# Four changes around TensorE in a four-layer graph network: degrees by quarters, layer 3's exponentials through DRAM, a weight and a bias moved to ScalarE, and a planner that prices changes of use by pairs

## The chip, the cores and the metric

The kernel runs on one core of a Trainium2 chip. The core has five engines with instruction queues of their own: TensorE (PE) multiplies matrices into accumulators (PSUM), VectorE (DVE) and ScalarE (ACT) do elementwise work and reductions, GpSimd (POOL) takes small powers here, and SyncE (SP) issues all transfers between DRAM and the on-chip memory (SBUF), which 16 DMA engines carry out. Engines wait for each other by semaphores. The metric is the device time of one execution in microseconds, the median of several runs.

## The reference, cut to what matters

64 graphs, independent of each other, with 256 nodes of 256 features and a 256 x 256 weighted adjacency each, pass through four layers. Each layer is `x = layernorm(x + layer(x, adj))`. All is float32.

```
layer 0: X, q, k = lrelu(x W_lin + b), lrelu(x W_q), lrelu(x W_k)          # 4 heads of 64
         A = adj * sigmoid(q k^T / 8); deg = sum over neighbours of A
         dis = deg^-0.5 where deg > 0, else 0; Y = layernorm(dis A dis X)
layer 1: masked attention, 8 heads of 32: q = x Wq + bq, softmax, v, Wo
layer 2: h = (eps x + adj x) W1 + b1                                       # 1024 wide
         h = silu(h * rsqrt(mean(h^2) + 1e-6) * rms_weight); h W2 + b2
layer 3: Wh = h W; e = leakyrelu(s1[i] + s2[j]), masked; softmax; attention Wh
         gelu(layernorm(...))
```

## The kernel before

**Staging.** A graph's arrays are tiles of 128 partitions. A 256 x 256 array is one tile of 128 x 512 (two blocks of 128 nodes, or of 128 features, side by side). All weights are loaded once. For each graph `graph()` (from L239) records some 300 operations, for all 64 graphs, and nothing is issued yet. An operation has an engine, a cost in ns, what it writes and reads, and for PE a *mode*: "full" (all of the array), "rows" (heads of 32 or 64 features on strips of rows, L433 and L515), "columns" (results of 32 or 64 partitions on strips of columns, L450, L476, L551) or "transpose" (a product with the identity).

**Order.** `Plan.order()` (L95 to L164) then plays the recorded operations through a model of the engines and writes down the order: at each step it takes, of all operations that have their inputs, the one that can start first. A change of PE's mode costs `CHANGE[mode]`, by the mode that is left (L23, L114). `AFTER` and `ITSELF` are the delays until another engine, or the same, may use a result. Buffers come from pools with fixed numbers of slots (`SLOTS`, L34: 42 of 128 x 516 words, 8 accumulators, 8 places in DRAM for bounces, and others), and an operation that needs a slot waits for a free one. ACT's tables (sigmoid, exponential, silu, gelu) are changed in *turns*, four for each round of graphs; layer 1 of a graph runs two rounds after its layer 0, layer 2 after five, layer 3 after seven (`ROUND`, L32). Loads may run at most `AHEAD` turns ahead (L29). So some eight graphs are in flight at different layers, and each engine gets one long fixed list that it works off in order. Every engine's list is fixed at build time; only semaphores hold it up.

**The parts that the change touches.** (Lines of the kernel before.)

- *Layer 0's degrees*, L448 to L464. VectorE has added the node blocks of A (`added`, two heads in each of two tiles). PE multiplies them by a 128 x 32 block of ones, one matmul of 256 columns for each head, into a strip of 32 partitions each (L450): in `ps`, the 32 partitions of a strip hold the same row of 256 degrees. ACT copies it to SBUF (L453), PE transposes it in two blocks (L458), and VectorE reads the degrees by node from every 32nd column of that accumulator (L462, L464), with POOL's power -0.5 (L463) between.
- *Layer 1's queries*, L499 to L502: PE's product and VectorE's addition of the bias per feature.
- *Layer 2*, L589 to L628. For eight blocks of 128 hidden features PE multiplies (L594), ACT adds the bias and brings the block to `hT` (L599), ACT squares two blocks at once (L602), VectorE adds the squares (L605, L607), PE takes the mean over features (L612), POOL the power (L616), and PE spreads the factors over the partitions of an accumulator `pr` (L621). VectorE multiplies each block by the RMS weight (a value per partition) and `pr` (L624), and ACT takes the silu of four blocks (L628). PE's second product (L637) follows.
- *Layer 3's exponentials*, L663 to L672: ACT, VectorE and ACT make `e`; PE transposes it in four blocks (L264), ACT copies the result to SBUF (L300), and PE multiplies it with `Wh` (L320, `ps<-v,eT`).
- *Transposition through DRAM*, `far_transposed` (L272): VectorE transposes the 32 x 32 blocks of a tile (L276), four transfers write them to DRAM (L282), four read them back with the blocks in their transposed places (L286), in runs of 32 words. Layer 3's input x3 goes this way in all but the last three graphs (L643).

Of the kernel before, what the change touches and what calls it, by code (L numbers as in the profile page):

```python
# [11 lines left out]
OP = mybir.AluOpType  # L12

P = 128
# [5 lines left out]
PE_MM, PE_TR = 432, 109  # L20
AFTER = {"PE": 230, "DVE": 150, "ACT": 190, "POOL": 180, "SP": 3000}
ITSELF = {"PE": 0, "DVE": 95, "ACT": 110, "POOL": 60, "SP": 0}
CHANGE = {"full": 0, "rows": 100, "columns": 140, "transpose": 60}  # L23
TABLE_LOAD = 1430

DMA_KB, DMA_SEEN = 4, 1900

WORDS = {"s": 516, "d": 1024, "b": 2048, "c": 32, "p": 512, "h": 1024}
AHEAD = 12  # L29
NEAR = 1, 1, 3  # L30

ROUND = 0, 2, 5, 7  # L32
# [43 lines left out]
class Plan:  # L76
# [9 lines left out]
    def op(self, engine, cost, fn, w=(), r=(), turn=None, mode="full", after=None, size=0):  # L86
        pair = lambda x: x if isinstance(x, tuple) else (x, None)
        w, r = [pair(x) for x in w], [pair(x) for x in r]
        op = Op(engine, cost, fn, w, r, self.graph, turn, mode, after, size)
        op.table = turn is not None and engine == "ACT"  # L90
        if op.table:
            self.turns[turn] = self.turns.get(turn, 0) + 1
        self.ops.append(op)

    def order(self):  # L95
        for i, op in enumerate(self.ops):
            op.index = i
        for op in reversed(self.ops):
            op.due = min((nxt.due for nxt in op.after), default=4 * (min(op.graph + ROUND[3], self.graphs - 1 + TAIL[3]) + 1))
            if op.turn is not None:  # L100
                op.due = min(op.due, op.turn)
        clock = {e: 0.0 for e in AFTER}
        self.free = {k: [(0.0, i) for i in range(n)] for k, n in SLOTS.items()}
        turns, left = sorted(self.turns), dict(self.turns)
        turn, loaded, mode, moved = 0, None, "full", 0.0
        ready = {op for op in self.ops if not op.waits}
        done = []
        self.busy = {e: 0.0 for e in AFTER}
        while ready:
            best = None  # L110
            for op in ready:
                if (op.due - AHEAD if op.first else op.turn or 0) > turns[turn]:
                    continue
                start = max(clock[op.engine] + (CHANGE[mode] if op.engine == "PE" and op.mode != mode else 0), op.ready)  # L114
                need = {}
                for v in op.values:
                    if v.slot is None:
                        need[v.kind] = need.get(v.kind, 0) + 1
                for kind, n in need.items():
                    free = self.free[kind]  # L120
                    if len(free) < n:
                        break
                    start = max(start, sorted(free)[n - 1][0])
                else:
                    key = start, op.due, op.graph, op.index
                    if best is None or key < best[0]:
                        best = key, start, op
            if best is None:
                raise RuntimeError(f"the plan is stuck at {len(done)} of {len(self.ops)}")
            _, start, op = best  # L130
            op.start = start
            ready.discard(op)
            if op.table and op.turn != loaded:
                op.start, loaded = op.start + TABLE_LOAD, op.turn
            if op.engine == "PE":
                mode = op.mode
            end = clock[op.engine] = op.start + op.cost
            op.landed = end + op.seen
            if op.engine == "SP":
                moved = max(moved, end) + op.size * DMA_KB  # L140
                op.landed = max(op.landed, moved + DMA_SEEN)
            self.busy[op.engine] += op.cost
            done.append(op)
            op.takes = [v for v in op.values if v.slot is None]
            for v in op.takes:
                self.free[v.kind].sort()
                v.slot = self.free[v.kind].pop(0)[1]
            for v in op.values:
                v.uses -= 1
                v.end = max(v.end, op.landed)  # L150
                if not v.uses:
                    self.free[v.kind].append((v.end, v.slot))
            for nxt in op.after:
                nxt.waits -= 1
                nxt.ready = max(nxt.ready, end + ITSELF[op.engine] if nxt.engine == op.engine != "SP" else op.landed)
                if not nxt.waits:
                    ready.add(nxt)
            if op.table:
                left[op.turn] -= 1
                while turn < len(turns) - 1 and not left[turns[turn]]:  # L160
                    turn += 1
        assert len(done) == len(self.ops)
        self.span = max(op.start + op.cost for op in done)
        return sorted(done, key=lambda op: op.start)  # L164
# [7 lines left out]
def weights(plan, nc, c, t):  # L172
# [38 lines left out]

    v = const("eps_id", [P, P])
    op("DVE", 200, lambda v=v: nc.vector.tensor_scalar(v.t, c.ident, c.eps2.t[:, 0:1], None, op0=OP.mult), [v], [c.eps2])


    ps, v = Value("p", "ps"), const("c1", [P, D])
# [22 lines left out]
def graph(plan, nc, c, t, out, b):  # L239
# [206 lines left out]
           [added[i]], [(att, 2 * i), (att, 2 * i + 1)])  # L446

    def fn(ps=ps):  # L448
        for h in range(H0):
            pe.matmul(ps.t[h * 32:(h + 1) * 32, :N], c.ones, two(added[h // 2])[:, h % 2], start=True, stop=True)  # L450
    op("PE", PE_MM, fn, [ps], added, mode="columns")
    deg = Value("s", "deg")
    op("ACT", 258, lambda ps=ps: act.copy(deg.t[:, :N], ps.t[:, :N]), [deg], [ps])  # L453
    pd = Value("p", "ps")

    def fn():
        for n in range(NB):
            pe.transpose(pd.t[:, n * P:(n + 1) * P], deg.t[:, n * P:(n + 1) * P], c.ident)  # L458
    op("PE", 2 * PE_TR, fn, [pd], [deg], mode="transpose")
    dp, dis = Value("c", "dp"), Value("c", "dis")  # L460
    D8 = lambda: pd.t[:, :N].rearrange("p (g k) -> p g k", k=32)[:, :, 0]
    op("DVE", 50, lambda: dve.tensor_scalar(dp.t[:, :8], D8(), TINY, None, op0=OP.max), [dp], [pd])  # L462
    op("POOL", 1610, lambda: pool.tensor_tensor(dp.t[:, :8], dp.t[:, :8], c.mhalf, OP.pow), [dp], [dp])  # L463
    op("DVE", 83, lambda: dve.scalar_tensor_tensor(dis.t[:, :8], D8(), 0.0, dp.t[:, :8], op0=OP.is_gt, op1=OP.mult),  # L464
       [dis], [pd, dp])
    by_head = lambda ap: ap.rearrange("p (g d) -> p g d", d=HD0)
    dis_b = lambda: dis.t[:, :8, None].to_broadcast([P, NB * H0, HD0])
# [15 lines left out]
    else:  # L483
# [13 lines left out]
    xT = copy(transposed(x), "xT")  # L497
    xb = plus_row(x, c.c1)
    ps = feature_major(c.w1_q, xT)  # L499
    qT1 = Value("s", "qT1")  # L500
    op("DVE", 602, lambda ps=ps: dve.tensor_tensor(two(qT1), two(ps), c.b1_q.t[:, :, None].to_broadcast([P, 2, N]), OP.add),
       [qT1], [ps, c.b1_q])  # L502

    kT1 = copy(feature_major(c.w1_k, xT), "kT1")
    v1 = copy(token_major(xT, lambda: c.w1_v.t, [c.w1_v]), "v1")
# [83 lines left out]
    for j in range(0, HB, 2):  # L589
        ps = Value("p", "ps", 2)  # L590
        for i in range(2):
            def fn(ps=ps, j=j, i=i):
                for k in range(DB):
                    pe.matmul(two(ps)[:, i, :], c.w2_1.t[:, k, (j + i) * P:(j + i + 1) * P], two(aggT)[:, k, :],  # L594
                              start=(k == 0), stop=(k == DB - 1))
            op("PE", 2 * PE_MM, fn, [(ps, i)], [aggT, c.w2_1])
        both = [(hT, j), (hT, j + 1)]
        for i in range(2):
            op("ACT", 357, lambda ps=ps, i=i, j=j: act.activation(  # L599
                Hb(j + i)[:, 0], two(ps)[:, i, :], AF.Identity, bias=c.b2_1.t[:, j + i:j + i + 1]), [(hT, j + i)], [(ps, i), c.b2_1])  # L600
        sq = Value("s", "sq")
        op("ACT", 520, lambda sq=sq, j=j: act.activation(two(sq), Hb(j, 2), AF.Square), [sq], both)  # L602
        sqs.append(sq)
        if len(sqs) > 1:
            op("DVE", 602, lambda a=sqs[0], sq=sq: dve.tensor_tensor(a.t, a.t, sq.t, OP.add), [sqs[0]], [sq, sqs[0]])  # L605
# [14 lines left out]
        for n in range(NB):  # L620
            pe.transpose(pr.t[:, n * P:(n + 1) * P], rs.t[:, n:n + 1].to_broadcast([P, P]), c.ident)  # L621
    op("PE", 2 * PE_TR, fn, [pr], [rs], mode="transpose")
    for j in range(HB):
        op("DVE", 391, lambda j=j: dve.scalar_tensor_tensor(  # L624
            Hb(j)[:, 0], Hb(j)[:, 0], c.r2.t[:, j:j + 1], pr.t[:, :N], op0=OP.mult, op1=OP.mult), [(hT, j)], [(hT, j), pr, c.r2])
        if j % 4 == 3:
            four = [(hT, i) for i in range(j - 3, j + 1)]
            op("ACT", 965, lambda j=j: act.activation(Hb(j - 3, 4), Hb(j - 3, 4), AF.Silu), four, four,  # L628
               turn=turn(2, SILU))
    ps = Value("p", "ps", 2)  # L630
    for n in range(NB):
        for half in range(2):
# [35 lines left out]
    r3 = Value("c", "r3")  # L668
    softmax(e, negmask, 1.0, e, lambda n: two(e)[:, n, :], lambda n: n, r3, lambda n: n, turn(3, EXP))
    op("DVE", 70, lambda: dve.reciprocal(r3.t[:, :NB], r3.t[:, :NB]), [r3], [r3])  # L670
    eT = copy(transposed(e), "eT")
    ps = token_major(eT, lambda: V3()[:, :, :D], [v3])  # L672
    y3 = Value("s", "y", 2)
    mv, m = stats(ps, r3)
# [91 lines left out]
```

## Time and profile before

The median of three runs is 2791.36 us (2789.9 to 2795.58). The profiled execution has a span of 2787.5 us and took 2789.26.

| view of the page | before |
|---|---|
| DMA, all queues | 546,947 packets, 473.08 MB, 58.4% of 16 engines in the transfers that SyncE issues |
| packets under 512 B | 177,376 |
| layer 1's exponentials and their sums, ACT L401 | 576.1 us busy, x1152 |
| layer 2's two products, PE L594 and L637 | 471.6 and 479.8 us busy |
| transfers to and from DRAM for x3, L282 and L286 | x244 each, 64 KB, 1.8 and 2.5 us from issue to landing |
| changes of ACT's table | 251, 1,283 ns each |

How to read it: a group's line gives the kernel line, engine and operation, what it writes and reads, shape and count; then busy time and mean duration in ns; then how long the engine had been idle just before these instructions, and what ended most of that. Durations of neighbouring instructions overlap on an engine, so the distance from one start to the next is often shorter than the duration. PEld are the loads of the stationary operand, which run beside PE's matmuls. A float32 matmul shows as two records; a transpose as one.

### The profile page before, as it was taken

The page shows a single profiled execution, that of the slowest core. Times are in us where ns is not written, and L with a number is a line of the kernel's source. Part 1 is how long each engine was busy: PE and PEld are TensorE (multiplying, and loading weights), DVE is VectorE, ACT ScalarE, POOL GpSimd, SP SyncE. Part 2 cuts the span into 40 slices and gives each one's busy share as a digit, 9 for nine tenths or more (in the row PEclk, how much of TensorE's full clock was granted, in tenths as well). Part 3 has the DMA queues.
Part 4 walks back from the last instruction along what each step waited for, and adds up shares of the span by engine and source line. Part 5 has one row for each costly group of instructions (what it writes and reads, how often), then busy time and mean ns, then how long its engine had stood idle before and what let it go on. Part 6 is the DMA issues. An engine that isn't in the chain of part 4 may idle for free.

```text
span 2787.5 us, 54969 instructions
## 1 busy us (share of the span) xinstructions
PE 2739.8 (98%) x17140; PEld 2191.9 (79%) x17140; DVE 2483.4 (89%) x7748; ACT 2138.6 (77%) x5064; POOL 582.3 (21%) x902
## 2 busy tenths in 40 slices
PE   8999999999999999999999999999999999999997
PEld 6777788787787877877787777787778877788776
DVE  5889999899988999899989988898989899899976
ACT  4778778788778787877777777778878777778775
POOL 1112222122121121221221221212212122122112
PEclk9999999999999999999999999999999999999999
DMA  5676756465663766565656655475665566566540
GB/s 152 193 198 177 209 161 198 148 183 159 200 168 107 219 188 184 155 177 170 192 152 183 196 164 147 139 206 152 197 174 167 155 191 182 159 195 183 158 133 20
DMA packets 546947, 473.08 MB, mean 170 GB/s; under 512 B 177376, under 2 KB 505952, under 8 KB 546656
## 3 DMA queue, kind: packets, MB, share of 16 engines
q1 hardware_dynamic: 546656, 469.58, 58.4%
q8 instruction: 137, 2.24, 0.4%
q14 instruction: 154, 1.26, 0.2%
HBM read 287.45 MB, written 181.93 MB: 168 GB/s over the span
## 4 chain that ended last, share of the span: by engine, by line
PE 87%; DVE 7%; ACT 3%; DMA 1%; issue 1%; POOL 1%; SPq 0%; DVEq 0%; POOLq 0%; ACTq 0%
PE ps L309 15%; PE ps L637 15%; PE ps L320 15%; PE ps L594 14%; PE ps L515 5%; PE ps L433 4%; PE ps L476 4%; PE ps L582 4%; PE av L551 4%; PE ps L652 3%; PE ps L264 2%; ACT e L401 1%; PE ps L450 1%; DVE eb L536 1%; DVE st L334 1%
## 5 line engine op out<-in xcount | busy, mean ns | idle before, releaser
L401 ACT ACTIVATE e<-e,low 128x256 f32<-128x256 f32 x1152 | 576.1, 502 | 74.6 <-DVE low L396 73.3
L637 PE MATMUL ps<-w,hT 128*128 128x256 f32 x2048 | 479.8, 382 | 5.5 <-ACT hT L628 5.5
L594 PE MATMUL ps<-aggT,w 128*128 128x256 f32 x2048 | 471.6, 382 | 2.8 <-DVE y L377 1.6
L346 POOL TENSOR_SCALAR mv<-mv 128x2 f32<-128x2 f32 x384 | 126.9, 331 | 1627.7 <-DVE mv L336 1108.8
L594 PEld LDWEIGHTS ps<-aggT,w 128*128 128x128 f32 x2048 | 381.5, 190 | 72.6 <-issue 8.3
L637 PEld LDWEIGHTS ps<-w,hT 128*128 128x128 f32 x2048 | 381.4, 190 | 67.5 <-issue 10.8
L396 DVE CUSTOM_DVE_ANT_0 e<-ps,adj 128x256 f32<-128x256 f32 x1024 | 361.5, 420 | 33.6 <-PE ps L515 27.0
L347 POOL TENSOR_TENSOR mv<-mv,mhalf 128x2 f32<-128x2 f32 x384 | 304.2, 792 | 32.0
L536 DVE STREAM_TRANSPOSE eb<-e 128x1024 f32<-128x1024 f32 x252 | 306.0, 1225 | 4.3 <-ACT e L401 4.2
L599 ACT ACTIVATE hT<-ps,b 128x256 f32<-128x256 f32 x512 | 229.0, 473 | 89.1 <-PE ps L594 61.7
L361 ACT ACTIVATE x<-y,mv 128x256 f32<-128x256 f32 x384 | 215.7, 597 | 67.3 <-DVE mv L357 59.9
L334 DVE BATCH_NORM_STATS2 st<-y 128x6 f32<-128x256 f32 x640 | 243.4, 412 | 1.2
L401 ACT ACTIVATION_READ_ACCUMULATOR e<-e,low 128x1 f32 x1152 | 220.8, 192 | 0.0
L624 DVE SCALAR_TENSOR_TENSOR hT<-hT,r,pr 128x256 f32<-128x256 f32 x512 | 206.0, 473 | 9.0 <-PE pr L621 9.0
L605 DVE TENSOR_TENSOR sq<-sq 128x512 f32<-128x512 f32 x192 | 130.8, 681 | 67.8 <-ACT sq L602 66.5
L439 DVE TENSOR_TENSOR att<-att,adjT 128x512 f32<-128x512 f32 x256 | 166.2, 676 | 2.5 <-ACT att L437 2.5
L602 ACT ACTIVATE sq<-hT 128x512 f32<-128x512 f32 x256 | 162.3, 634 | 1.2
L515 PE MATMUL ps<-kT,qT 32*128 32x256 f32 x2048 | 148.1, 398 | 0.0
L463 POOL TENSOR_TENSOR dp<-dp,mhalf 128x8 f32<-128x8 f32 x64 | 108.3, 1692 | 185.7 <-DVE dp L462 137.9
L628 ACT ACTIVATE hT<-hT 128x1024 f32<-128x1024 f32 x128 | 130.7, 1052 | 18.7 <-DVE hT L624 14.0
L437 ACT ACTIVATE att<-ps 128x512 f32<-128x512 f32 x256 | 132.2, 602 | 11.1 <-PE ps L637 5.6
L309 PE MATMUL ps<-x0T,w_q 128*128 128x256 f32 x512 | 128.9, 387 | 5.9 <-DMA x0T<-in_xT 5.9
(113 smaller groups left out, 5523.5 us busy)
## 6 DMA issues: line engine op xcount, KB each, us to landing
far<-eb SPq DMA_DIRECT2D x252, 512.0 KB, 3.4
eT<-far SPq DMA_DIRECT2D x1008, 128.0 KB, 3.7
adj<-in_adj SPq DMA_DIRECT2D x128, 256.0 KB, 4.8
x0T<-in_xT SPq DMA_DIRECT2D x64, 256.0 KB, 3.6
adjT<-in_adjT SPq DMA_DIRECT2D x64, 256.0 KB, 4.6
x<-in_x SPq DMA_DIRECT2D x64, 256.0 KB, 4.9
adj<-in_adjT SPq DMA_DIRECT2D x64, 256.0 KB, 3.4
rb<-far SPq DMA_DIRECT2D x512, 32.0 KB, 1.9
```

What stands on the lines that cost most here:

```text
L309: pe.matmul(two(ps)[:, o, :], w.t[:, k, o * P:(o + 1) * P], two(xT)[:, k, :], start=(k == 0), stop=(k == DB - 1))
L320: pe.matmul(two(ps)[:, n, :], two(xT)[:, k, n * P:(n + 1) * P], w()[:, k, :], start=(k == 0), stop=(k == DB - 1))
L334: op("DVE", 328, lambda n=n: dve.bn_stats(st.t[:, 6 * n:6 * n + 6], two(src)[:, n, :]), [(st, n)], [(src, n)])
L347: pool.tensor_tensor(m()[:, :, 2], m()[:, :, 2], c.mhalf[:, :NB], OP.pow)
L361: op("ACT", 492, lambda n=n: act.activation(two(dst)[:, n, :], two(src)[:, n, :], AF.Identity, bias=m()[:, n, 0:1], scale=m()[:, n, 2:3]), ...
L396: op("DVE", 345, lambda n=n: dve.tensor_tensor_reduce(out=E(n), in0=two(logits)[:, n, :], in1=two(negmask)[:, n, :], scale=-scale, scalar= ...
L401: op("ACT", 491, lambda n=n: act.activation(E(n), E(n), AF.Exp, bias=low.t[:, n:n + 1], scale=-1.0, accum_out=r.t[:, col(n):col(n) + 1]), ...
L515: pe.matmul(two(pss[i])[:, n, :], two(qT1)[s, hq, n * P:(n + 1) * P], two(kT1)[s, hq, :], start=True, stop=True)
L536: op("DVE", 1155, lambda e=e, eb=eb: dve.transpose(eb.t.rearrange("p (b g i) -> p g b i", b=4, i=32), e.t.rearrange("p (g b i) -> p g b i" ...
L594: pe.matmul(two(ps)[:, i, :], c.w2_1.t[:, k, (j + i) * P:(j + i + 1) * P], two(aggT)[:, k, :], start=(k == 0), stop=(k == DB - 1))
L599: op("ACT", 357, lambda ps=ps, i=i, j=j: act.activation(Hb(j + i)[:, 0], two(ps)[:, i, :], AF.Identity, bias=c.b2_1.t[:, j + i:j + i + 1]) ...
L637: pe.matmul(two(ps)[:, n, :], Hb(j)[:, 0, n * P:(n + 1) * P], c.w2_2.t[:, j, :], start=(j == 0), stop=(j == HB - 1))
```

## The change

Its parts, each to take work off PE or VectorE, or to let the planner see what PE really spends:

1. *Degrees by quarters.* The ones multiply a quarter of the columns (32 of every 128) at a time, eight matmuls of 128 columns, and each quarter's degrees go to its own strip of 32 partitions. VectorE's transposition of 32 x 32 blocks then puts each degree on its node's partition. ACT's copy and PE's two transposes go.
2. *Layer 3's exponentials* go through `far_transposed` in all but the last three graphs, instead of through PE and ACT.
3. *RMS weight by ACT.* ACT squares from the accumulator, with the bias, and brings the block to `hT` with scale (the weight) and bias (bias times weight, a new constant `br2`). VectorE's product with `pr` then takes four blocks in one instruction.
4. *Queries' bias by ACT*, in two instructions in place of VectorE's one.
5. *The planner.* Changes of use are priced by pair of modes. In choosing, a change out of strips is held back by `STAY`. Loads may run 14 turns ahead, not 12.

```diff
-CHANGE = {"full": 0, "rows": 100, "columns": 140, "transpose": 60}
+CHANGE = {("full", "rows"): 92, ("full", "columns"): 92, ("rows", "full"): 315, ("columns", "full"): 240,
+          ("rows", "columns"): 212, ("columns", "rows"): 136, ("rows", "rows"): 103, ("columns", "columns"): 70, ("transpose", "rows"): 92,
+          ("transpose", "columns"): 92, ("rows", "transpose"): 260, ("columns", "transpose"): 192}
...
-AHEAD = 12
+AHEAD = 14
+STAY = 200
...
-                start = max(clock[op.engine] + (CHANGE[mode] if op.engine == "PE" and op.mode != mode else 0), op.ready)
+                start = clock[op.engine]
+                if op.engine == "PE" and mode in ("rows", "columns") and mode != op.mode:
+                    start += STAY - 60 * (op.mode == "transpose")
+                start = max(start, op.ready)
...
             if op.engine == "PE":
+                op.start = max(op.start, clock["PE"] + CHANGE.get((mode, op.mode), 0))
                 mode = op.mode
...
-        for h in range(H0):
-            pe.matmul(ps.t[h * 32:(h + 1) * 32, :N], c.ones, two(added[h // 2])[:, h % 2], start=True, stop=True)
+        for i in range(2):
+            for g in range(4):
+                pe.matmul(ps.t[g * 32:(g + 1) * 32, i * P:(i + 1) * P], c.ones,
+                          added[i].t.rearrange("p (m g t) -> p m g t", g=4, t=32)[:, :, g], start=True, stop=True)
...
-    op("ACT", 258, lambda ps=ps: act.copy(deg.t[:, :N], ps.t[:, :N]), [deg], [ps])
...
-            pe.transpose(pd.t[:, n * P:(n + 1) * P], deg.t[:, n * P:(n + 1) * P], c.ident)
-    op("PE", 2 * PE_TR, fn, [pd], [deg], mode="transpose")
+    pd = Value("s", "deg")
+    op("DVE", 340, lambda ps=ps: dve.transpose(pd.t[:, :N], ps.t[:, :N]), [pd], [ps])
...
-    op("DVE", 602, lambda ps=ps: dve.tensor_tensor(two(qT1), two(ps), c.b1_q.t[:, :, None].to_broadcast([P, 2, N]), OP.add),
-       [qT1], [ps, c.b1_q])
+    for o in range(2):
+        op("ACT", 357, lambda ps=ps, o=o: act.activation(
+            two(qT1)[:, o, :], two(ps)[:, o, :], AF.Identity, bias=c.b1_q.t[:, o:o + 1]), [(qT1, o)], [(ps, o), c.b1_q])
...
         for i in range(2):
-            op("ACT", 357, lambda ps=ps, i=i, j=j: act.activation(
-                Hb(j + i)[:, 0], two(ps)[:, i, :], AF.Identity, bias=c.b2_1.t[:, j + i:j + i + 1]), [(hT, j + i)], [(ps, i), c.b2_1])
-        sq = Value("s", "sq")
-        op("ACT", 520, lambda sq=sq, j=j: act.activation(two(sq), Hb(j, 2), AF.Square), [sq], both)
+            op("ACT", 357, lambda ps=ps, sq=sq, i=i, j=j: act.activation(
+                two(sq)[:, i, :], two(ps)[:, i, :], AF.Square, bias=c.b2_1.t[:, j + i:j + i + 1]), [(sq, i)], [(ps, i), c.b2_1])
+            op("ACT", 491, lambda ps=ps, i=i, j=j: act.activation(
+                Hb(j + i)[:, 0], two(ps)[:, i, :], AF.Identity, bias=c.br2.t[:, j + i:j + i + 1],
+                scale=c.r2.t[:, j + i:j + i + 1]), [(hT, j + i)], [(ps, i), c.br2, c.r2])
...
-        op("DVE", 391, lambda j=j: dve.scalar_tensor_tensor(
-            Hb(j)[:, 0], Hb(j)[:, 0], c.r2.t[:, j:j + 1], pr.t[:, :N], op0=OP.mult, op1=OP.mult), [(hT, j)], [(hT, j), pr, c.r2])
+        op("DVE", 1130, lambda j=j: dve.tensor_tensor(
+            Hb(j, 4), Hb(j, 4), pr.t[:, None, :N].to_broadcast([P, 4, N]), OP.mult), four, [*four, pr])
...
-    eT = copy(transposed(e), "eT")
+    eT = copy(transposed(e), "eT") if b >= plan.graphs - NEAR[2] else far_transposed(e, "eT3")
```

More of the change, by code (lines that the diff above doesn't have):

```diff
@@ L213, in weights @@
     op("DVE", 200, lambda v=v: nc.vector.tensor_scalar(v.t, c.ident, c.eps2.t[:, 0:1], None, op0=OP.mult), [v], [c.eps2])
+    v = const("br2", [P, 8])
+    op("DVE", 60, lambda v=v: nc.vector.tensor_tensor(v.t, c.b2_1.t, c.r2.t, OP.mult), [v], [c.b2_1, c.r2])
     ps, v = Value("p", "ps"), const("c1", [P, D])
@@ L448, in fn @@
     def fn(ps=ps):
-        for h in range(H0):
-            pe.matmul(ps.t[h * 32:(h + 1) * 32, :N], c.ones, two(added[h // 2])[:, h % 2], start=True, stop=True)
+        for i in range(2):
+            for g in range(4):
+                pe.matmul(ps.t[g * 32:(g + 1) * 32, i * P:(i + 1) * P], c.ones,
+                          added[i].t.rearrange("p (m g t) -> p m g t", g=4, t=32)[:, :, g], start=True, stop=True)
     op("PE", PE_MM, fn, [ps], added, mode="columns")
[L452 to L458, printed above, removed]
-    op("PE", 2 * PE_TR, fn, [pd], [deg], mode="transpose")
+    pd = Value("s", "deg")
+    op("DVE", 340, lambda ps=ps: dve.transpose(pd.t[:, :N], ps.t[:, :N]), [pd], [ps])
     dp, dis = Value("c", "dp"), Value("c", "dis")
-    D8 = lambda: pd.t[:, :N].rearrange("p (g k) -> p g k", k=32)[:, :, 0]
-    op("DVE", 50, lambda: dve.tensor_scalar(dp.t[:, :8], D8(), TINY, None, op0=OP.max), [dp], [pd])
+    D8 = lambda: pd.t[:, :N].rearrange("p (h n k) -> p n h k", n=NB, k=32)[:, :, :, 0]
+    op("DVE", 50, lambda: dve.tensor_scalar(dp.t[:, :8].rearrange("p (n h) -> p n h", n=NB), D8(), TINY, None, op0=OP.max), [dp], [pd])
     op("POOL", 1610, lambda: pool.tensor_tensor(dp.t[:, :8], dp.t[:, :8], c.mhalf, OP.pow), [dp], [dp])
-    op("DVE", 83, lambda: dve.scalar_tensor_tensor(dis.t[:, :8], D8(), 0.0, dp.t[:, :8], op0=OP.is_gt, op1=OP.mult),
+    op("DVE", 83, lambda: dve.scalar_tensor_tensor(
+        dis.t[:, :8].rearrange("p (n h) -> p n h", n=NB), D8(), 0.0, dp.t[:, :8].rearrange("p (n h) -> p n h", n=NB), op0=OP.is_gt, op1=OP.mult),
        [dis], [pd, dp])
@@ L499, in graph @@
     ps = feature_major(c.w1_q, xT)
-    qT1 = Value("s", "qT1")
-    op("DVE", 602, lambda ps=ps: dve.tensor_tensor(two(qT1), two(ps), c.b1_q.t[:, :, None].to_broadcast([P, 2, N]), OP.add),
-       [qT1], [ps, c.b1_q])
+    qT1 = Value("s", "qT1", 2)
+    for o in range(2):
+        op("ACT", 357, lambda ps=ps, o=o: act.activation(
+            two(qT1)[:, o, :], two(ps)[:, o, :], AF.Identity, bias=c.b1_q.t[:, o:o + 1]), [(qT1, o)], [(ps, o), c.b1_q])
     kT1 = copy(feature_major(c.w1_k, xT), "kT1")
@@ L596, in graph @@
             op("PE", 2 * PE_MM, fn, [(ps, i)], [aggT, c.w2_1])
-        both = [(hT, j), (hT, j + 1)]
+        sq = Value("s", "sq", 2)
         for i in range(2):
-            op("ACT", 357, lambda ps=ps, i=i, j=j: act.activation(
-                Hb(j + i)[:, 0], two(ps)[:, i, :], AF.Identity, bias=c.b2_1.t[:, j + i:j + i + 1]), [(hT, j + i)], [(ps, i), c.b2_1])
-        sq = Value("s", "sq")
-        op("ACT", 520, lambda sq=sq, j=j: act.activation(two(sq), Hb(j, 2), AF.Square), [sq], both)
+            op("ACT", 357, lambda ps=ps, sq=sq, i=i, j=j: act.activation(
[3 more added lines that the diff above has]
+                scale=c.r2.t[:, j + i:j + i + 1]), [(hT, j + i)], [(ps, i), c.br2, c.r2])
         sqs.append(sq)
@@ L622, in graph @@
     op("PE", 2 * PE_TR, fn, [pr], [rs], mode="transpose")
-    for j in range(HB):
-        op("DVE", 391, lambda j=j: dve.scalar_tensor_tensor(
-            Hb(j)[:, 0], Hb(j)[:, 0], c.r2.t[:, j:j + 1], pr.t[:, :N], op0=OP.mult, op1=OP.mult), [(hT, j)], [(hT, j), pr, c.r2])
[L626 to L629, printed above, removed]
+    for j in range(0, HB, 4):
+        four = [(hT, i) for i in range(j, j + 4)]
+        op("DVE", 1130, lambda j=j: dve.tensor_tensor(
+            Hb(j, 4), Hb(j, 4), pr.t[:, None, :N].to_broadcast([P, 4, N]), OP.mult), four, [*four, pr])
+        op("ACT", 965, lambda j=j: act.activation(Hb(j, 4), Hb(j, 4), AF.Silu), four, four, turn=turn(2, SILU))
     ps = Value("p", "ps", 2)
```

## The prediction

> **What bounds the kernel now.** I read the busy line and the slices of the page first, then the chain that ended last, then the groups of instructions by line, and last the timeline of TensorE.
>
> ```profile
> PE 2739.8 (98%) x17140; PEld 2191.9 (79%) x17140; DVE 2483.4 (89%) x7748; ACT 2138.6 (77%) x5064; POOL 582.3 (21%) x902
> ...
> PE   8999999999999999999999999999999999999997
> ...
> PEclk9999999999999999999999999999999999999999
> ...
> PE 87%; DVE 7%; ACT 3%; DMA 1%; issue 1%; POOL 1%; SPq 0%; DVEq 0%; POOLq 0%; ACTq 0%
> ```
>
> TensorE is full in every slice but the first and the last, at full clock, and 87% of the chain is its own work. A busy PE in these records need not be at its peak, so I counted its work in slots. The timeline gives the slot lengths:
>
> ```profile
> 1401.41 1.95 PE L476 MATMUL ps<-att,v 128*64 128x256 f32 x16
> 1403.29 0.64 PE L450 MATMUL ps<-added,ones 128*32 128x256 f32 x8
> 1403.86 1.99 PE L320 MATMUL ps<-w_o,yT 128*128 128x256 f32 x8
> 1405.69 1.89 PE L309 MATMUL ps<-x0T,w_k 128*128 128x256 f32 x8
> 1407.42 1.11 PE L320 MATMUL ps<-v,eT 128*128 128x256 f32 x4
> ...
> 1411.40 0.38 PE L621 MATMUL pr<-ident,rs 128*128 128x128 f32 x2
> 1411.62 0.38 PE L458 MATMUL ps<-ident,deg 128*128 128x128 f32 x2
> 1411.84 0.27 PE L558 MATMUL ps<-ident,r 128*16 128x128 f32 x1
> 1411.95 1.91 PE L652 MATMUL ps<-w,xT 128*128 128x258 f32 x8
> ```
>
> The reader is to take the distances between starts, not the durations. L309's 8 records take 1407.42 - 1405.69 = 1.73 us, 0.216 us each, and a 256-column matmul is two records. A transpose takes 0.109 us (L621 to L458 is 0.22 for two), though its record lasts 273 ns. Matmuls on row or column strips run two or four abreast and count once. Per graph that is 72 full matmuls x 0.432 = 31.1 us, four strip blocks (L433, L515, L476, L551) x 1.73 = 6.9, L450 0.43, 15.75 transposes (1008 in 64 graphs) x 0.109 = 1.72, and L612 four records x 0.112 = 0.45: 40.6 us, x 64 = 2,600 us.
>
> The same distances show what a change of use costs. Above, L450's 8 records need 0.43 us but L320 starts 0.57 after it, and L320's own block is stretched from 1.73 to 1.83. Medians over the whole trace, of what the first two intervals after a change take too long: full to rows 197 ns, rows to full 212, full to columns 130, columns to full 217, columns to another column block 123, rows or columns to a transpose 164, full to a transpose and back about 0. With the counts of the order, these make 117 us. From the first matmul (5.9 us) to the start of the last (16.5 us before the end) lie 2,765 us, so 2,765 - 2,600 - 117 = 48 us are left for real waits. By place about 13 of them are in the first 140 us and 14 in the last 210 us. The steady stretch has nearly none, so time comes from removing PE slots, changes of use, or not at all.
>
> **What the Trainium skill says.** (1) "TensorEngine Tiling (Array Packing)", Key Properties: changing the tiling mode, not just the tile, drains TensorE. The trace agrees: about 200 ns in and 210 out, and nothing between full and transpose. (2) "ScalarE: Activation LUTs", What ACT_TABLE_LOAD costs: every [128,1] pointer operand adds about 93 ns to an ACTIVATE. Its formula gives about 493 ns with one and 586 with two at 256 elements; the rows have 473 (L599) and 597 (L361). (3) "VectorE: DVE Perf Modes", The three transpose paths: VectorE transposes 32 x 32 blocks only, which is why the change sends quarters of columns to quarters of partitions, and why layer 3 needs DRAM to place its blocks.
>
> **The change part by part.** The rows used:
>
> ```profile
> L264 PE MATMUL ps<-ident,e 128*128 128x128 f32 x288 | 44.2, 276 | 2.3 <-ACT e L401 2.0 <-DVE y L487 0.2
> L458 PE MATMUL ps<-ident,deg 128*128 128x128 f32 x128 | 24.7, 275 | 0.0
> L453 ACT COPY deg<-ps 128x256 f32<-128x256 f32 x64 | 23.9, 374 | 55.1 <-PE ps L450 54.7
> L501 DVE TENSOR_TENSOR qT<-ps,b_q 128x512 f32<-128x512 f32 x64 | 43.3, 677 | 11.3 <-PE ps L309 10.6
> L300 ACT COPY eT<-ps 128x512 f32<-128x512 f32 x64 | 37.5, 587 | 28.4 <-PE ps L264 28.1
> L624 DVE SCALAR_TENSOR_TENSOR hT<-hT,r,pr 128x256 f32<-128x256 f32 x512 | 206.0, 473 | 9.0 <-PE pr L621 9.0
> L599 ACT ACTIVATE hT<-ps,b 128x256 f32<-128x256 f32 x512 | 229.0, 473 | 89.1 <-PE ps L594 61.7 <-PE ps L637 27.1
> L602 ACT ACTIVATE sq<-hT 128x512 f32<-128x512 f32 x256 | 162.3, 634 | 1.2
> L361 ACT ACTIVATE x<-y,mv 128x256 f32<-128x256 f32 x384 | 215.7, 597 | 67.3 <-DVE mv L357 59.9 <-issue 4.9 <-DVE r L670 0.8
> ```
>
> *Degrees by quarters.* L458's 128 transposes go: 128 x 0.109 = 14.0 us of PE slots, all on the path. The ones matmuls become eight of 128 columns, four abreast as before: the same 0.43 us if strip loads keep up. A load record of 32 columns lasts 110 ns and a group's slot is now 109, where it was 216. Bounds: nothing, or one slot of 0.03 us more in each of four groups, 0.12 x 64 = 8 us. The loads of four strips start within 20 ns of each other here, so I take 1 us. ACT loses L453. VectorE gains one 128x256 transpose, some 0.34 us to its next start (L276's 512 columns take 0.63, half is 0.32). The accumulator is freed after it instead of being held through POOL's 1.6 us power.
>
> *Layer 3's exponentials through DRAM*, 61 of 64 graphs: 61 x 4 = 244 transposes x 0.109 = 26.6 us of PE slots go, on the path; so do 61 ACT copies and the accumulators for them. VectorE gains 61 x 0.63 = 38 us. SyncE gains 488 issues. By the same queue's rows, a write lands 1.8 us and a read 2.5 us after issue, and issuing takes 433 and 622 ns: 0.7 + 4 x 0.43 + 1.8 + 4 x 0.62 + 2.5 = 9 us from exponential to matmul. The planner allows for 11.6. Other graphs' matmuls hide it: their order is planned with it. The 128 B packets of the like transfer for x3 take 3.7% of the 16 engines, its 512 B ones half of 4.6%, so the DMA goes from 58% to about 64%; SyncE's issuing from 1,477 us to about 1,740, 63%. Behind a waiting transfer in that queue stand other graphs' loads and bounces; PE would wait for them, at no measured price, so it is a rival below.
>
> *RMS weight and queries' bias by ACT.* The distances between starts: L599 357 ns, L361 with two pointers 494, L602 520. ACT gains 512 x 357 - 256 x 520 = 50 us (squares from the accumulator), 512 x (494 - 357) = 70 us (scale as well as bias) and 128 x 357 = 46 us (queries), and loses 64 x 264 = 17 (L453) and 61 x 466 = 28 (copies): +121 on 2,041, so 2,162 us, or 79% of the new time. VectorE loses L501, 64 x 601 = 38 us, and L624, 512 x 392 = 201. It gains 128 products of 1,024 elements: the 256- and 512-element ones start 332 and 602 ns apart, so 602 + 540 = 1,142 ns, 146 us. With 38 + 22 for the transposes, VectorE loses 33 us and stays at 89%. Both lie beside PE, so I cost them at nothing for the time.
>
> *Changes of use by pairs*, a longer look-ahead (14 turns of ACT for 12) and a bar to leaving strips early. The planner's old prices made one visit to row strips 100 ns; its new ones make it 92 + 315 = 407, the trace 197 + 212 = 409. What it does with them can be counted in the built orders: full to rows 156 then 159, rows to full 155 then 119, rows to transpose 17 then 59, full to columns 80 then 93, columns to full 84 then 61, columns to transpose 19 then 40. At the measured prices all changes together make 117.0 us before and 116.0 after: 1 us. Table loads stay at 251.
>
> *The sum.* 14.0 + 26.6 - 1 + 1 = 40.6 us, and of the waits at L458 and at L264's exponentials, some 4 us outside the warm-up: 45. From the median of 2,791.4 that is **2,747 us**.
>
> **The rivals.** (a) *ACT becomes the bound of layer 2.* Eight blocks take PE 6.9 us; ACT's work on them grows from 8 x 357 + 4 x 520 = 4.9 us to 8 x (357 + 494) = 6.8, with each accumulator held for both reads. Against it speaks that L599 now waits 89 us for PE, nearly never the other way (5.5 us of PE's own waits are for ACT's silu), and that 21% of ACT stay free; for it, that exponentials of other graphs queue between these. If half of the added 1.9 us showed, 64 x 0.95 = 60: 2,807 us, slower. (b) *The SyncE queue or late transposed tiles cost some 0.4 us a graph*, 61 x 0.4 = 25: 2,772. At 0.7 us a graph there is no change. (c) *The better plan also takes waits away*: half of the 48 us: 2,723. That waits are rare between 140 and 2,570 us speaks against more.
>
> **How the numbers follow.** Forecast (2,735 to 2,760) 0.66; (c) 0.12; (b) between 2,760 and 2,785 0.12; no change 0.03; (a) or worse (b), slower, 0.07. The range from 2,726 to 2,774 leaves out the slower cases, half of (c) and a few of (b). Faster 0.90, same 0.03, slower 0.07.
>
> **What would show it.** Right: no L458 group and 44 transposes of e (32 of layer 1, 12 of layer 3), PE near 2,700 busy and still 98%, ACT near 79%, VectorE 89%, and the PE waits no longer. Wrong: PE slots waiting on ACT's squares or scaled copies, on eT's landing, or the degree block stretched past 0.6 us.

## The result, and the profile after

The changed kernel takes 2,766.5 us in the median (2,761.1 to 2,770.1, six runs), against 2,791.3 before: ratio 0.9908, 95% interval 0.9892 to 0.9923, some 25 us less. Forecast were 2,747 us (44 less) and a range from 2,726 to 2,774. The direction was right and the time lies in the range, but only 25 of 44 us came, and it lies outside the band that the prediction held most likely (2,735 to 2,760), in the one it gave to rival (b). The question for the runs was where the other 19 went.

The page after, the same four lines as before:

```profile
PE 2703.5 (98%) x17280; PEld 2160.5 (78%) x17280; DVE 2443.0 (89%) x7426; ACT 2224.2 (81%) x5323; POOL 574.6 (21%) x902
...
PE   8999999999999999999999999999999999999997
...
PEclk9999999999999999999999999999999999999999
...
PE 75%; DVE 10%; ACT 6%; DMA 4%; SPq 2%; issue 2%; POOL 0%; DVEq 0%; POOLq 0%; ACTq 0%
```

PE is busy 36 us less and still 98% of the span, so it remains the bound. The chain tells that something is less tidy: PE's own share falls from 87% to 75%, and VectorE, ACT, DMA and SyncE's queue take its place. The chain passes through them where PE waited. The shares are no measure of lost time: 12% of the span would be 330 us, and PE's idle time rose by 8 (below).

The groups that took the place of those in the prediction (groups by line and shape; busy us, mean ns | idle before):

```profile
L275 PE MATMUL ps<-ident,e 128*128 128x128 f32 x44 | 6.4, 276 | 0.9 <-ACT e L412 0.9
L462 PE MATMUL ps<-added,ones 128*32 128x128 f32 x1024 | 40.7, 277 | 0.0
L466 DVE STREAM_TRANSPOSE deg<-ps 128x256 f32<-128x256 f32 x64 | 27.6, 432 | 0.3 <-PE ps L591 0.2
L635 DVE TENSOR_TENSOR hT<-hT,pr 128x1024 f32<-128x1024 f32 x128 | 149.7, 1209 | 5.3 <-PE pr L631 5.3
L610 ACT ACTIVATE hT<-ps,br,r 128x256 f32<-128x256 f32 x512 | 288.8, 575 | 10.2 <-PE ps L645 6.7 <-PE ps L603 3.5
L608 ACT ACTIVATE sq<-ps,b 128x256 f32<-128x256 f32 x512 | 242.0, 480 | 82.7 <-PE ps L603 73.0 <-DMA yT<-far 2.3 <-DMA far<-rT 1.7
```

Of 288 transposes of exponentials 44 are left, L458 has no group, and the degree block has twice the records for the same time. The timeline shows that for one graph:

```profile
1771.34 1.95 PE L484 MATMUL ps<-att,v 128*64 128x256 f32 x16
1773.22 0.64 PE L462 MATMUL ps<-added,ones 128*32 128x128 f32 x16
1773.79 1.99 PE L331 MATMUL ps<-w_o,yT 128*128 128x256 f32 x8
```

From start to start it takes 0.57 us, as it did before between the same two neighbours: the loads of four strips keep up with slots of 109 ns.

What PE waited for, from the views of waits of PE, before and then after (us in total, times, longest):

```profile
PE ps L309 <- DMA x0T<-in_xT: 5.9, 1, 5.9
PE ps L637 <- ACT hT L628: 5.5, 2, 3.0
PE ps L320 <- DVE yT L568: 2.8, 2, 2.3
PE ps L320 <- ACT eT L300: 2.6, 4, 1.0
```

```profile
PE ps L320 <- DMA x0T<-in_xT: 6.1, 1, 6.1
PE ps L645 <- ACT hT L637: 4.8, 1, 4.8
PE ps L524 <- ACT kT L311: 4.2, 7, 1.2
PE ps L660 <- DMA xT<-far: 2.9, 2, 1.7
```

The start-up load and waits of some 5 us for the silu are common to both. New are many small waits: for the keys' copy on ACT, and for x3's way through DRAM. No single one is large. All lines of the two views together come to 30.1 and 38.0 us: 6.0 more for ACT, 3.3 more for DMA, 1.4 less for VectorE. So I took PE's time apart as in the prediction for every run: slots by the counts and lengths given there, changes of use by the same medians, and the waits as what is left between PE's first and last start. These are us of the profiled run of each kernel, beside the median of its timed runs. Slots and changes of use are counts at fixed prices; only their sum with the waits is measured, and what a slot is worth is tested by f_pe below.

| kernel | median | span | slots | changes of use | waits |
|---|---|---|---|---|---|
| before | 2,791 | 2,787.5 | 2,600.1 | 116.5 | 48.5 |
| changed | 2,766 | 2,759.3 | 2,559.8 | 115.6 | 60.9 |
| changed, PE's delay 240 for 230 (n_pe) | 2,810 | 2,809.7 | 2,559.8 | 120.6 | 108 |
| changed, ACT's delay 185 for 190 (n_act) | 2,786 | 2,778.8 | 2,559.8 | 117.3 | 78 |
| changed, three costs as measured (calib) | 2,806 | 2,806.6 | 2,559.8 | 118.2 | 105 |
| before, PE's delay 240 (n_before) | 2,795 | 2,795.6 | 2,600.1 | 113.0 | 59 |
| before, new planner alone (p_alone) | 2,806 | 2,802.4 | 2,600.1 | 110.7 | 69 |
| changed order, transposes put back (f_pe) | 2,795 | 2,798.1 | 2,600.3 | 115.1 | 59 |
| changed order, no scale on ACT (f_act) | 2,760 | 2,757.7 | 2,559.8 | 115.6 | 58.5 |
| changed order, pieces of 2 KB (f_dma) | 2,758 | 2,753.9 | 2,559.8 | 115.6 | 55 |
| degrees undone (u_degree) | 2,836 | 2,835.7 | 2,573.5 | 122.6 | 116 |
| layer 3 undone (u_far) | 2,802 | 2,800.7 | 2,586.4 | 114.7 | 79 |
| RMS weight undone (u_rms) | 2,813 | 2,813.4 | 2,559.8 | 112.4 | 118 |
| planner undone (u_plan) | 2,821 | 2,820.4 | 2,559.8 | 123.4 | 116 |

From before to changed the span falls by 28.2: slots -40.3, changes of use -0.9, waits +12.4, start and end +0.6. The medians differ by 3 us less, because the six runs of the changed kernel lie in two groups of three, at 2,761 to 2,763 us and at 2,770, and the profiled one is the fastest of them. (The expectations below were written with 53 us of waits for the kernel before and 65 for the changed one, where the table has 48.5 and 60.9.)

The waits of the table are not idle time alone. The traces' clock records hold stretches of 3.4 or 6.8 us in which TensorE was granted half of its clock: between the first and the last matmul, two in the kernel before, two in the changed one, seven in n_pe and thirteen in u_plan. In these four traces PE is idle for 25.6, 33.2, 68.0 and 69.8 us, and loses 3.3, 4.5, 13.2 and 28.2 us at half clock (half of its busy time in these stretches); what then remains, 18 to 27 us, is intervals that are a little too long. In all 14 traces PE was idle for at least 0.8 of the 3.4 us just before each such stretch. So the cost of a wait needn't end with the wait.

### The profile page after: what moved, and what is told of

The parts are those of the page before. It is cut to its first block, busy times and chain, and to the rows that moved or that the text cites. A ratio compares the mean times of both kernels' runs of the same rounds, so it can differ in the third digit from the quotient of the medians.

```text
span 2759.3 us, 56034 instructions
## 1 busy us (share of the span) xinstructions
PE 2703.5 (98%) x17280; PEld 2160.5 (78%) x17280; DVE 2443.0 (89%) x7426; ACT 2224.2 (81%) x5323; POOL 574.6 (21%) x902
## 3 DMA queue, kind: packets, MB, share of 16 engines
q1 hardware_dynamic: 710624, 501.59, 65.9%
## 4 chain that ended last, share of the span: by engine, by line
PE 75%; DVE 10%; ACT 6%; DMA 4%; SPq 2%; issue 2%; POOL 0%; DVEq 0%; POOLq 0%; ACTq 0%
PE ps L331 13%; PE ps L320 13%; PE ps L645 13%; PE ps L603 11%; PE ps L444 4%; PE ps L524 4%; PE ps L484 3%; PE av L560 3%; PE ps L660 3%; PE ps L591 3%; ACT e L412 2%; DVE e L407 2%; DVE st L345 1%; DMA eT<-far 1%; PE ps L275 1%
## 5 line engine op out<-in xcount | busy, mean ns | idle before, releaser
L603 PE MATMUL ps<-aggT,w 128*128 128x256 f32 x2048 | 476.4, 382 | 3.8 <-DVE low L407 1.9
L603 PEld LDWEIGHTS ps<-aggT,w 128*128 128x128 f32 x2048 | 379.7, 190 | 69.4 <-DVE low L407 11.7
L608 ACT ACTIVATE sq<-ps,b 128x256 f32<-128x256 f32 x512 | 242.0, 480 | 82.7 <-PE ps L603 73.0
L358 POOL TENSOR_TENSOR mv<-mv,mhalf 128x2 f32<-128x2 f32 x384 | 298.6, 778 | 32.0
L610 ACT ACTIVATE hT<-ps,br,r 128x256 f32<-128x256 f32 x512 | 288.8, 575 | 10.2 <-PE ps L645 6.7
L372 ACT ACTIVATE x<-y,mv 128x256 f32<-128x256 f32 x384 | 217.3, 602 | 50.9 <-DVE mv L368 48.9
L635 DVE TENSOR_TENSOR hT<-hT,pr 128x1024 f32<-128x1024 f32 x128 | 149.7, 1209 | 5.3 <-PE pr L631 5.3
L524 PEld LDWEIGHTS ps<-kT,qT 32*128 32x128 f32 x2048 | 97.9, 184 | 47.5 <-issue 23.3
```

Source lines behind the costliest of these rows:

```text
L358: pool.tensor_tensor(m()[:, :, 2], m()[:, :, 2], c.mhalf[:, :NB], OP.pow)
L524: pe.matmul(two(pss[i])[:, n, :], two(qT1)[s, hq, n * P:(n + 1) * P], two(kT1)[s, hq, :], start=True, stop=True)
L608: op("ACT", 357, lambda ps=ps, sq=sq, i=i, j=j: act.activation(two(sq)[:, i, :], two(ps)[:, i, :], AF.Square, bias=c.b2_1.t[:, j + i:j + i ...
L610: op("ACT", 491, lambda ps=ps, i=i, j=j: act.activation(Hb(j + i)[:, 0], two(ps)[:, i, :], AF.Identity, bias=c.br2.t[:, j + i:j + i + 1], ...
```

## The experiments

### Undoing one part at a time

For the degrees and layer 3 the old operations were put back into the changed kernel:

```
u_degree: the ones in four matmuls of 256 columns, ACT's copy, PE's two transposes, as before
u_far:    -eT = copy(transposed(e), "eT") if b >= plan.graphs - NEAR[2] else far_transposed(e, "eT3")
          +eT = copy(transposed(e), "eT")
u_rms:    bias by ACT, squares of two blocks from hT, eight products of hT, weight and pr on VectorE, as before
u_plan:   the old CHANGE and its use, no STAY, AHEAD = 12
```

> The changed kernel with layer 0's degrees as before (ACT's copy and PE's two transposes); all else as changed. Theory of slots: time is PE's slots plus changes of use, and waits stay. 128 transposes come back, 14.0 us, and the new order has 123.1 us of changes of use against 116.0 (counted pairs at the medians of the trace): +21 us, about 2,787. Theory of waits (ACT's added work holds PE up): the same plus a little for 17 us more ACT work, 2,787 to 2,792. Theory of re-planning (any edit shuffles the lists and moves the time by some 10 us): anywhere from 2,775 to 2,797.

> The changed kernel with layer 3's exponentials transposed by PE and copied by ACT in all 64 graphs; all else as changed. Slots: 244 transposes come back, 26.6 us, changes of use 115.2 against 116.0: +26 us, 2,792. If the way through DRAM is what brought PE's new waits (late tiles or the SyncE queue), these 10 to 17 us go again and only some 10 to 16 us are added: 2,776 to 2,782. Re-planning: 2,782 to 2,802.

> The changed kernel with the RMS weight applied by VectorE, eight instructions a graph, and ACT's squares from SBUF as before; all else as changed. No PE slot changes; changes of use 112.8 against 116.0. Slots alone: -3 us, 2,763. Theory of waits: ACT loses some 97 us of work and accumulators come free earlier, so most of the 17 us of new waits in the steady stretch go: 2,748 to 2,755. Rival, VectorE (89% busy) is the engine that the waits hang on and the move relieved it: with 57 us more VectorE work, 2,770 to 2,785.

> All four kernel edits, with the planner as before (old prices of modes, no STAY, 12 turns ahead). Slots: the same; changes of use 123.7 against 116.0: +8 us, 2,774. If the better prices also take waits away, as the plan's clock runs truer: 2,780 or more. If the planner's part is worth nothing or its longer look-ahead hurts: 2,760 to 2,768.

Measured: 2,835.5 (ratio to before 1.0163, 1.0141 to 1.0186), 2,801.8 (1.0039, 1.0024 to 1.0053), 2,812.5 (1.0076, 1.0060 to 1.0093) and 2,821.3 us (1.0108, 1.0090 to 1.0126). Every one is slower than the kernel before. u_degree and u_rms are so by more than any theory had it; u_far lies at the edge of re-planning, and u_plan fits its second theory, which had no upper end. By the counts, slots and changes of use are 13.7 and 7.0 us more than in the changed kernel for u_degree, and slots 26.6 more for u_far; what was not foreseen is 18 to 57 us of further waits (in u_plan 24 of 55 are time lost at half clock). They appear even in u_rms, which takes work off ACT and leaves PE's slots alone. The rival named for it, VectorE, is not excluded by this run: PE's waits for VectorE come to 32.7 us in its view, against 8.5 in that of the changed kernel. But they are 20.1 in that of n_pe below, with the work unchanged. Parts with nothing in common all seemed indispensable. That is no measure of the parts: each edit also makes the planner draw a new list for every engine. So the next runs changed the list alone, or the work alone.

### The list changed, the work kept

```
n_pe:  -AFTER = {"PE": 230, ...    +AFTER = {"PE": 240, ...
n_act: -"ACT": 190                 +"ACT": 185
```

> The changed kernel; in the planner alone one delay differs: a result of PE may be used 240 ns after it, not 230. The work is the same and nothing in the machine changes; the lists come out in another order (changes of use 121.0 us against 116.0). Theory of the drawn plan (how little PE waits depends on the one plan that was kept, and any other plan of these operations has 85 to 125 us of waits): 2,785 to 2,825. Theory of causes (the four undone versions were slow for what was undone): 2,766 + 5 = 2,771, at most 2,778.

> The same with another neutral shift: a result of ACT may be used after 185 ns, not 190 (changes of use 117.8). Drawn plan: 2,785 to 2,825. Causes: 2,768, at most 2,775.

Measured: 2,809.9 us (1.0060, 1.0043 to 1.0076) and 2,786.2 us (0.9982, 0.9974 to 0.9989). A number in the planner that means nothing to the machine costs 44 and 20 us. The shifted plan's waits, from the view of PE's waits of n_pe:

```profile
PE ps L462 <- DVE added L456: 10.3, 11, 2.5
PE ps L645 <- ACT hT L637: 7.6, 5, 4.3
PE ps L320 <- DMA x0T<-in_xT: 6.3, 1, 6.3
PE ps L591 <- ACT x L372: 5.4, 7, 1.7
PE ps L603 <- ACT v L664: 5.0, 1, 5.0
```

In the changed kernel PE never waited before L462. Here the list puts the degree block too close behind VectorE's sum eleven times. The operations and their lengths are the same; their places differ. The fifth line shows what can follow a wait (PE's timeline, and the view by stretches of the same place, with PEclk, DMA share and GB/s as its last three columns):

```profile
1054.68 1.03 PE L660 MATMUL ps<-w,xT 128*128 128x258 f32 x4
1060.70 3.78 PE L603 MATMUL ps<-aggT,w 128*128 128x256 f32 x8 [4.98 <-ACT v L664]
1064.27 2.05 PE L645 MATMUL ps<-w,hT 128*128 128x256 f32 x8
```

```profile
1057.80:1064.60 6.80, 3.90 (x9) 3.19 (x10) 0.92 (x4) 0.76 (x3) 0.00 (x0) 0.50 0.94 275
```

After 4.98 us of waiting, L603's 8 records take 1064.27 - 1060.70 = 3.57 us, where 8 such records take 1.73 at full clock. Of the 47 us by which n_pe's waits exceed those of the changed kernel, 35 are more idle time of PE and 9 more time lost at half clock.

The same shift in the kernel before, and the new planner alone on the old operations:

> The kernel before with the same neutral shift in its planner as in the first shifted plan (PE's results after 240 ns, not 230); the work is the same, changes of use 113.5 us against 117.0. Drawn plan: the kernel before is as special as the changed one, and its shifted plan has 80 to 125 us of waits instead of 53: 2,815 to 2,860. If only the changed kernel is fragile (its ACT is fuller): 2,785 to 2,800.

> The kernel before with the new planner alone (prices by pairs, STAY, 14 turns ahead). Changes of use 111.3 us against 117.0. Slots: 2,786. Drawn plan: 2,785 plus 20 to 60 us, 2,805 to 2,845. If the truer prices take waits away as well: below 2,775.

Measured: 2,795.2 us (1.0012, 1.0006 to 1.0019) and 2,805.6 us (1.0049, 1.0034 to 1.0064). The first is against the plain form of the theory of the drawn plan: the old operations took the shift with 4 us more, the new ones with 44. One shift is little to judge by; it suggests that the old set of operations forgives more, and does not show why. In the second, one plan as well, the new planner is no gain by itself: changes of use fall by 5.8 us, and waits rise by 21.

A plan with costs nearer to the trace:

```
calib: ACT's scaled pass 491 -> 449 ns, the degrees' transposition 340 -> 363, issue of a transposed read 420 -> 622
```

> The changed kernel with three of the planner's costs set to what the trace of the changed kernel shows: the scaled pass of ACT 449 ns (491 planned), the degrees' transposition 363 (340), the issue of a transposed read 622 (420). Changes of use 118.6 us. If waits come from a plan that differs from the machine: below 2,760. Drawn plan: 2,775 to 2,825, since it is one more plan.

Measured: 2,806.5 us (1.0048, 1.0031 to 1.0064), waits 105 us. Truer costs for these three did not help; it was one more plan. Of five plans of the changed operations (changed, n_pe, n_act, calib, and u_plan with the old planner), one beats the kernel before by 25 us, one by 5, and three lose 15 to 31. The means of the medians are 2,798 us for these five and 2,797 for the three plans of the old operations (before, n_before, p_alone), with 94 and 59 us of waits. So the 25 us are the difference of two particular plans. That the new operations have more waits in most plans, which would eat their saved slots, fits these numbers, but eight plans from different planners do not show it.

### The list kept, the work changed

These three have the changed kernel's order, operation for operation, on every engine; only what is issued at a place differs.

```
f_pe:  def token_major(xT, w, r=(), spare=0): ...
       +    for k in range(spare):
       +        pe.transpose(two(ps)[:, n, k * P:(k + 1) * P], c.ident, c.ident)   # then overwritten by the product
       (spare 1 for layer 0's values, 2 for layer 3's last product in 61 graphs)
f_act: -AF.Identity, bias=c.br2..., scale=c.r2...   +AF.Identity, bias=c.br2...
f_dma: for eT3 alone, -dst "q (g a i)" <- F(a) "q (g i)"   +dst.t[32 * a:32 * a + 32] <- F(a) "(j x) w -> j (x w)"
```

> The changed kernel in its order; as many transposes of the identity as the change took away (2 in each graph, 4 more in 61 graphs, 372 in all) stand ahead of layer 0's values and layer 3's last product, into accumulators that these products then overwrite. Nothing is waited for that was not before. Slots: 372 x 0.109 = 40.6 us, 2,807. If PE's 65 us of waits take some of it up, as waits behind which PE is idle anyway: 2,780 to 2,795.

Measured: 2,795.1 us (1.0016, 1.0008 to 1.0024). Putting 40.6 us of transposes back costs 29 us by the medians and 38.8 us by the profiled spans, in which slots rise by 40.5 and waits fall by 1.8. Each order's runs spread over some 10 us, which is the gap between the two figures. So in this order a PE slot is worth about 0.7 of itself by the medians and 0.96 in the traces: the part of the theory of slots that matters stands. With the old number of slots, the changed kernel is 4 us slower than the kernel before: between these two plans the removed slots are all of the gain, and the rest of the change, its new list included, costs a little.

> The changed kernel in exactly its order on every engine; only the scale by the RMS weight is left out of ACT's second pass over each block (the plan still counts it). ACT loses about 93 ns in each of 512 instructions, 48 us. If ACT's added work is what holds PE up: half or more of the 27 us of waits for ACT go, 2,745 to 2,755. If the waits come from the order and not from ACT's amount of work: 2,763 to 2,767.

Measured: 2,759.6 us (0.9888, 0.9873 to 0.9903). ACT loses 48 us of work and the median falls by 7, between the two theories and nearer to the second; the profiled spans differ by only 1.6 us, and PE's waits for ACT fall from 19.9 to 17.2 us in its view. ACT's amount of work matters by a seventh of its size at most.

> The changed kernel in exactly its order; layer 3's exponentials are read back from DRAM in pieces of 2 KB instead of 128 B, so that they land in the wrong places (the blocks' transposition is left out). The same number of issues and bytes, 125,000 packets of 128 B fewer. If the new traffic of small packets or SyncE's longer issue is what delays PE: 2,750 to 2,758. If the way through DRAM is hidden: 2,763 to 2,768.

Measured: 2,757.9 us (0.9877, 0.9862 to 0.9892), 9 us less and at the upper end of the first theory (5.4 us less by the profiled spans). PE's waits in its trace:

```profile
PE ps L321 <- DMA x0T<-in_xT: 6.4, 1, 6.4
PE ps L646 <- ACT hT L638: 4.8, 1, 4.8
PE ps L525 <- ACT kT L312: 3.0, 6, 0.7
PE ps L485 <- DVE v L477: 1.7, 1, 1.7
```

The line for x3's transfers is gone (2.9 us; f_act and f_pe still have 2.7 and 3.0), though x3's own transfers are unchanged: the exponentials' reads held them up. The way through DRAM is thus not hidden altogether. Whether packets or issuing did it is not told apart: with the larger pieces SyncE's median issue of such a read falls from 621 to 412 ns as well, 53 us in all. The interval of f_act overlaps that of the changed kernel and the interval of f_dma touches it, so 7 and 9 us are sizes with an error of some 4 us.

No version beat the changed kernel with the whole computation in it. That pieces larger than 128 B for layer 3, by another way of placing the blocks, would gain some of the 9 us is a guess that was not tried.

## Why the prediction was right or wrong, point by point

- *TensorE is the bound, and slots are what counts.* Right, in a given order. PE stays at 98%, and f_pe prices 40.6 us of slots at 29 to 39 us in a fixed order.
- *Degrees by quarters, 14.0 us, and the block with strip loads at 1 us.* The transposes are gone as counted; the block takes 0.57 us between the same neighbours, as before, so next to nothing of the 1 us came and the bound of 8 us was far too wide. VectorE's transposition starts its successor after 363 ns, for 340.
- *Layer 3 through DRAM, 26.6 us, hidden.* The transposes are gone as counted. "Other graphs' matmuls hide it" was too strong: f_dma puts 5 to 9 us on the reads in pieces of 128 B, by their packets or by their issuing. The DMA share came to 65.9%, for 64%, and SyncE's issuing to 1,759 us, for 1,740. This is rival (b) at 0.09 to 0.15 us a graph, where it was priced at 0.4.
- *ACT's and VectorE's work costed at nothing.* ACT rose to 2,133 us by starts (2,162 foreseen), and to 81% of the span by the busy line (79% foreseen): the scaled pass takes 449 ns from start to start when it reads the accumulator, not 494. That is still 92 more than with one pointer, and agrees with the 93 ns that the Trainium skill states for each pointer operand ("ScalarE: Activation LUTs", What ACT_TABLE_LOAD costs). Costing it at nothing was wrong by 2 to 7 us for the scale alone, near the noise. Rival (a), half of the added time showing, would have been 60 us and did not come.
- *Changes of use, -1 us.* The count came out for before against after (116.5 and 115.6), at the prices of the prediction. The comparison behind the planner's part is another: with the old planner the new operations have 123.4.
- *Of the waits some 4 us less.* This step failed, and it is the term that was mis-sized: waits rose by 12.4 us, 16 us off. I treated the waits as belonging to the operations that I removed. The rows of the prediction do not even hold 4 us: PE's idle time is 0.0 us before L458 and 2.3 before L264's exponentials. How long PE waits depends on the order, which is drawn anew: the runs with changed lists have 78 to 108 us with exactly the same work.
- *Rival (c), the better plan takes waits away:* the reverse, in p_alone as in the result. But within the new operations u_plan, with the old planner, has 116 us of waits against 61. Whether the prices or the draw did that can't be told from one plan each.
- *The number.* That the time lies in the range owes something to luck. Of the five plans of the changed operations only the kept one is in it, and nothing on record says how that one came to be kept.

What stays open: how much of the 12 us of added waits is ACT's load, how much DMA traffic and how much the draw. f_act and f_dma are of the right size to make it up by their medians (7 and 9 us), but not by their spans (1.6 and 5.4), were not run together, and each alone is near the error. Whether the changed operations wait more than the old ones in most plans is open too.

## What to carry to other kernels

Where an engine is full for the whole span, count its slots by start-to-start distances and its changes of use by pairs; then test what a slot is worth (here 29 to 39 us for 40.6). In a kernel whose order a planner draws, an edit is two changes, the work and the list; try a neutral shift of the planner before crediting an edit with the difference, and test the work by itself in a fixed order. Read the granted clock beside the waits: time lost at half clock looks like waiting in a count of slots. Work that is "hidden" on an engine at 80% cost at most a seventh of its size here.

## What the runs showed of the hardware that was not expected

A scaled and biased ACT pass over 256 elements starts its successor after 449 ns when it reads an accumulator (L610) and after 493 when it reads SBUF (L372). Ones on four column strips run at full rate down to slots of 109 ns (0.57 us for the block with either slot). A kernel that keeps TensorE 97% busy still had thirteen stretches of half the granted clock (u_plan, mean clock 0.986), for two in the kernel before (0.997). And the same order of the same kernel spreads over some 10 us from run to run (2,761 to 2,770 for the changed kernel, 2,791 to 2,802 for f_pe), where the kernel before stays within 8 in 33 runs.
